# All embedding gathers on GpSimd, with seven tiles for gathered rows instead of two

## The chip, the cores and the metric

The kernel runs on one core of a Trainium2 chip. The metric is the device time of one execution in microseconds (us). Such a core has five engines that run side by side: TensorE (PE in the profile: matrix products and transposes), VectorE (DVE), ScalarE (ACT), GpSimd (POOL) and SyncE (SP, which here only issues transfers). Transfers between the chip's memory and the core's on-chip memory are done by 16 DMA engines; SyncE, ScalarE and GpSimd each have a queue on which they issue them.

## The reference, cut to what matters

A spiking recommender: each of 1024 users has 50 items, the rows of an embedding table that belong to them are averaged as a running prefix, normalised over the batch, run through a leaky integrate-and-fire neuron, and the mean spike count is scored against the whole table.

```python
emb = emb_table.at[0].set(0.0)             # 100001 x 128
e = emb[seq]                               # seq: 1024 x 50
prefix = jnp.cumsum(e, axis=1)
denom = jnp.minimum(t_idx[None, :], lengths[:, None])
uF = prefix / denom[:, :, None]
mean, var = uF.mean(axis=0), uF.var(axis=0)     # over the batch
y = (uF - mean) * lax.rsqrt(var + BN_EPS) * gamma + beta

def step(v, x):                            # scanned over the 50 steps
    v = v + (x - v) / TAU
    spike = (v - V_TH >= 0)
    return v - spike * V_TH, spike

scores = spikes.mean(axis=0) @ emb.T       # 1024 x 100001
```

## The kernel before

The kernel has two stages. The first computes the spike counts, 128 features by 1024 users; the second multiplies them with the whole table and writes 409.6 MB of scores.

**First stage, 50 steps.** Step t needs the rows of the table that the 1024 users have at place t. `gather(t)` (L201) takes a tile of 128 x 1024 and issues eight indirect transfers from GpSimd, one for each block of 128 users: each fetches 128 rows of 128 numbers, one row into each partition. The tiles come from the pool `gather`, which has two buffers. For four of the steps, 44 to 47, the first of the eight blocks is not gathered by GpSimd: it lies in a tile of its own, `aside[t]` (128 x 128). These four tiles are filled early by SyncE (L184 to L197): for each of the 128 partitions it reads four indices into registers and issues four transfers of one row (512 transfers of 0.5 KB), behind the loads of the indices, lengths and constants and the first six groups of table rows on the same queue. The gather loop then starts at block 1 for these steps (`range(t in aside, NB)`).

In the loop over t (L300), `gather(t + 1)` is issued first. TensorE transposes the eight blocks of step t and adds them onto the running prefix, which stays in two PSUM banks, `pre` (L313). For each half of the users VectorE scales the prefix by the length (L322) and takes its statistics (L323). Both halves' statistics give the mean and variance (L333), ScalarE and a few small VectorE instructions the scale (L337 to L352), ScalarE the normalised value (L338, L356), and VectorE the neuron's step, spike and reset (L343, L359, L365). TensorE adds a correction for item 0 (L270) and sums the spikes (L281). Step t + 1 can't have its neuron's step before step t has, so these form a recurrence beside the gathers. The order of work on each engine is that of the program; waits between engines follow from the tiles that are read and written.

At the end of steps 42 and 44 (L371 to L373) the first two blocks of 1024 table rows are prepared for the second stage: TensorE transposes them, ScalarE writes a rounded copy `hi`, VectorE the remainder `lo`. The four tiles for these, `hi0`, `lo0`, `hi1` and `lo1` (128 x 1024, pool `embT`), are taken at the start of the program (list `free`, L76) and are not used before step 42. In the last step VectorE computes the counts, and the first two blocks of scores are multiplied, scaled and stored (L396 to L408), the first of them in a tile of the pool `gather`.

At the start two more tiles of the pool `gather` serve other ends: `isz` (where an item is 0, L217) and `rb` (the lengths' reciprocals, L239), each transposed once by TensorE.

**Second stage.** For chunks of 2 to 6 blocks of 1024 table rows and for each of eight blocks of users, TensorE multiplies counts with `hi` and `lo`, VectorE and ScalarE take turns at moving the products to an output tile, and SyncE stores it (L427 to L493). The output tiles of the second stage lie where the tiles of the first stage lay.

Of the kernel before, what the change touches and what calls it, by code (L numbers as in the profile page):

```python
# [12 lines left out]
F32 = mybir.dt.float32  # L13
BF16 = mybir.dt.bfloat16
F32R = mybir.dt.float32r
# [5 lines left out]
P = 128  # L21
BN_EPS = 1e-5
V_TH = 1.0
HALF = 1024
KQ = HALF // P
BANK = 512
# [8 lines left out]
def rec_kernel(  # L35
# [9 lines left out]
    nc = tc.nc  # L45
    B, T = seq.shape
    N, D = table.shape
    NB = B // P
# [24 lines left out]
    rows = {}  # L73
    split = {}

    free = [  # L76
        [embp.tile([P, HALF], F32R, tag=f"{x}{i}", name=f"{x}_{i}") for x in ("hi", "lo")] for i in range(2)
    ]

    def size(q):  # L80
        return min(HALF, N - q * HALF)
# [79 lines left out]
    with ExitStack() as ph:  # L161
# [1 line left out]
        lp = ph.enter_context(tc.tile_pool(name="lif", bufs=2))  # L163
        sp = ph.enter_context(tc.tile_pool(name="stats", bufs=3))
        up = ph.enter_context(tc.tile_pool(name="uF", bufs=2))
        gp = ph.enter_context(tc.tile_pool(name="gather", bufs=2))
        accp = ph.enter_context(tc.tile_pool(name="acc", bufs=1, space=bass.MemoryType.PSUM))
        vp = ph.enter_context(tc.tile_pool(name="v", bufs=1, space=bass.MemoryType.PSUM))

# [11 lines left out]

        aside = {}  # L184
        for t0, many in ((T - 6, 4),):
            for t in range(t0, t0 + many):
                aside[t] = once.tile([P, P], F32, tag=f"aside{t}", name=f"aside_{t}")
            for p in range(P):
                _, items = nc.values_load_multi_w_load_instructions(
                    idx[p : p + 1, 0, t0 : t0 + many],  # L190
                    engines=[mybir.EngineType.SP],
                    min_val=0,
                    max_val=N - 1,
                    skip_runtime_bounds_check_because="items are rows of the table; the transfer checks its own bounds",
                )
                for j, item in enumerate(items):
                    nc.sync.dma_start(out=aside[t0 + j][p : p + 1, :], in_=table[bass.ds(item, 1), :])  # L197

        es = {}

        def gather(t):  # L201
            es[t] = gp.tile([P, B], F32, tag="e", name=f"e_{t}")
            for n in range(t in aside, NB):
                nc.gpsimd.indirect_dma_start(  # L204
                    out=es[t][:, n * P : (n + 1) * P],
                    out_offset=None,
                    in_=table,
                    in_offset=bass.IndirectOffsetOnAxis(ap=idx[:, n, t : t + 1].bitcast(U32), axis=0),
                )

        make_identity(nc, ident)
        gather(0)

        isz = gp.tile([P, NB, P], F32, tag="e", name="isz")  # L217
        nc.vector.memset(isz, 0.0)
        for u in (0, P // 2):
            nc.vector.tensor_single_scalar(isz[:, :, u : u + T], idx, 0.0, ALU.is_equal)  # L220
# [15 lines left out]
        rl = once.tile([P, NB], F32, tag="rl", name="rl")  # L236
        nc.vector.tensor_copy(rl, len_i)
        nc.vector.reciprocal(rl, rl)
        rb = gp.tile([P, NB, P], F32, tag="e", name="rb")  # L239
        nc.vector.tensor_copy(rb, rl.unsqueeze(2).to_broadcast([P, NB, P]))  # L240
        rps = vp.tile([P, B], F32, tag="v0", name="rps")
        for n in range(NB):
# [56 lines left out]
        l = only(1)  # L299
        for t in range(T):  # L300
            last = t == T - 1
            if t + 1 < T:
                gather(t + 1)
            e = es.pop(t)
            if last:
                s = lp.tile([P, B], BF16, tag="s", name=f"s_{t - 1}")
                nc.vector.tensor_single_scalar(s, v, V_TH, ALU.is_ge)
                nc.vector.tensor_tensor(negv, s, v, ALU.subtract)
            uF = up.tile([P, B], F32, tag="uF", name=f"uF_{t}")
            bs = sp.tile([P, B // BANK, 6], F32, tag="bs", name=f"bs_{t}")  # L310
            for h, cs in enumerate(halves):
                for k in range(0, BANK, P):
                    nc.tensor.matmul(  # L313
                        pre[h][:, k : k + P],
                        lhsT=aside[t] if h == k == 0 and t in aside else e[:, h * BANK + k : h * BANK + k + P],
                        rhs=ident,
                        start=False,
                        stop=last,
                        is_transpose=True,
                        skip_group_check=True,  # L320
                    )
                nc.vector.scalar_tensor_tensor(uF[:, cs], rlen[:, cs], 1.0 / (t + 1), pre[h], ALU.max, ALU.mult)  # L322
                nc.vector.bn_stats(bs[:, h, :], uF[:, cs])  # L323
            if not last:
                correct(t + 1, l)
            else:

                counted(t - 1, s)
                count = once.tile([P, B], F32, tag="zT", name="count")
                for h, cs in enumerate(halves):  # L330
                    nc.scalar.copy(count[:, cs], sums[h])
            mv = sp.tile([P, 2], F32, tag="mv", name=f"mv_{t}")
            nc.vector.bn_aggr(mv, bs.rearrange("p h s -> p (h s)"))  # L333


            r = sp.tile([P, 1], F32, tag="r", name=f"r_{t}")
            nc.scalar.activation(r, mv[:, 1:2], AF.Sqrt, bias=eps)  # L337
            nc.scalar.activation(uF, uF, AF.Identity, bias=mv[:, 0:1], scale=-1.0)  # L338


            if t and not last:
                s = lp.tile([P, B], BF16, tag="s", name=f"s_{t - 1}")
                nc.vector.tensor_single_scalar(s, v, V_TH, ALU.is_ge)  # L343
                counted(t - 1, s)

            nc.vector.reciprocal(r, r)
            q = sp.tile([P, 1], F32, tag="q", name=f"q_{t}")
            nc.vector.tensor_mul(q, r, r)
            nc.vector.scalar_tensor_tensor(q, mv[:, 1:2], BN_EPS, q, ALU.add, ALU.mult)
            nc.vector.tensor_scalar(q, q, -0.5, 1.5, ALU.mult, ALU.add)  # L350
            a = sp.tile([P, 1], F32, tag="a", name=f"a_{t}")
            nc.vector.tensor_scalar(a, q, r, hgb[:, 0:1], ALU.mult, ALU.mult)  # L352


            def x(vt, cs):
                nc.scalar.activation(vt, uF[:, cs], AF.Identity, bias=hgb[:, 1:2], scale=a)  # L356

            def step(vt, cs):
                nc.vector.scalar_tensor_tensor(vt, negv[:, cs], -0.5, vt, ALU.mult, ALU.add)  # L359

            if not last:
                vt = vp.tile([P, B], F32, tag=f"v{t % 2}", name=f"v_{t}")
                x(vt, whole)
                if t:
                    nc.vector.tensor_tensor(negv, s, v, ALU.subtract)  # L365
                step(vt, whole)
                v = vt
                if t + 2 < T:
                    l = only(t + 2)

                if t in (T - 8, T - 6):  # L371
                    q = (t - T + 8) // 2
                    prepare(q, vp.tile([P, HALF], F32, tag="v1", name=f"pt_{q}"))  # L373


# [20 lines left out]


        po1 = vp.tile([P, HALF], F32, tag="v0", name="po_0_1")
        for q, (pool, tag, po) in enumerate(((gp, "e", sums), (up, "uF", [po1[:, cs] for cs in halves]))):
            o = pool.tile([P, HALF], F32, tag=tag, name=f"o_0_{q}")  # L400
            for h, cs in enumerate(halves):
                product(po[h], q, 0, h * BANK, BANK)
# [110 lines left out]
```

## Time and profile before

| | |
|---|---|
| median of three runs | 1776.87 us |
| lowest and highest run | 1771.08 and 1780.48 us |
| profiled execution, span from first to last instruction | 1569.9 us |
| time of the profiled execution beyond its span | not given by the page |
| instructions | 14231 |
| TensorE, VectorE, ScalarE, GpSimd busy | 1153.1, 940.7, 630.6, 374.6 us |
| gathers on GpSimd | 396, 373.9 us busy, 944 ns each |
| mean transfer rate | 311 GB/s |
| HBM read and written | 77.69 and 409.60 MB |

All of these except the runs' times come from one execution, recorded by the hardware profiler. The page cuts its span into 40 slices and gives the busy share of each engine in tenths. It lists the costliest groups of instructions by line, and the chain of work that ended last: from the last instruction back, at each step to what released it. "issue" is time in which an engine waited for nothing that the profile shows. A row in order of time has the start, the duration, the engine, the line, what is written and read, and in brackets the idle time before it and what ended it.

### The profile page before, as it was taken

How to read it: one execution, taken by the hardware profiler on the slowest of the kernel's cores; microseconds unless marked ns; L12 is line 12 of the kernel's file. 1: busy time of each engine (PE TensorE's matmuls, PEld its weight loads, DVE VectorE, ACT ScalarE, POOL GpSimd, SP SyncE). 2: the span in 40 equal slices, each digit the busy share in tenths (PEclk: the TensorE clock that was granted, in tenths of full speed). 3: DMA queues.
4: the chain of work that ended last, by engine and by line, in shares of the span. 5: the costliest groups of instructions: out<-in, count | busy, mean ns of one | idle time of the engine just before them, and what ended most of it. 6: DMA issues, size and time to landing. Idle time of an engine off the chain costs nothing.

```text
span 1569.9 us, 14231 instructions
## 1 busy us (share of the span) xinstructions
PE 1153.1 (73%) x4548; PEld 822.3 (52%) x4548; DVE 940.7 (60%) x1161; ACT 630.6 (40%) x700; POOL 374.6 (24%) x402
## 2 busy tenths in 40 slices
PE   4555555555556988899878788887788888788784
PEld 2222222222233766677666666666666666666563
DVE  4777777777778665576545555555555545555453
ACT  2322222222233554465444444444444444444342
POOL 6777777777775000000000000000000000000000
PEclk7555555555555999999999988999999998989998
DMA  9622222222222999999999999999999999999998
GB/s 342 245 55 53 55 54 54 54 53 54 52 53 64 399 411 420 420 393 428 425 432 427 429 428 424 418 422 424 428 413 420 415 424 429 421 423 409 394 423 354
DMA packets 54600, 488.25 MB, mean 311 GB/s; under 512 B 12443, under 2 KB 13756, under 8 KB 33276
## 3 DMA queue, kind: packets, MB, share of 16 engines
q1 hardware_dynamic: 33008, 429.03, 65.1%
q0 software_dynamic: 12672, 25.98, 6.2%
q10 hardware_dynamic: 8844, 32.33, 5.2%
q8 instruction: 36, 0.59, 0.1%
q14 instruction: 40, 0.33, 0.1%
HBM read 77.69 MB, written 409.60 MB: 310 GB/s over the span
## 4 chain that ended last, share of the span: by engine, by line
DMA 52%; POOL 17%; PE 11%; issue 9%; ACT 5%; DVE 4%; DVEq 0%; ACTq 0%; SPq 0%; POOLq 0%
DMA scores<-o 49%; POOL e L204 17%; PE po L149 9%; ACT o L473 5%; DMA e<-in_L_rec_emb_table,idx 3%; DVE o L471 2%; PE pt L119 1%; DVE bs L323 1%; DVE uF L322 0%; DVE s L343 0%; PE pre L313 0%; PE sums L281 0%; DMA idx<-in_r_seq 0%; ACT hi L141 0%; ACT pairs L141 0%
## 5 line engine op out<-in xcount | busy, mean ns | idle before, releaser
L471 DVE TENSOR_SCALAR o<-po 128x1024 f32<-128x1024 f32 x391 | 463.5, 1220 | 351.8 <-DMA scores<-o 323.4
L473 ACT ACTIVATE o<-po 128x1024 f32<-128x1024 f32 (+1 forms) x391 | 387.9, 1018 | 547.8 <-DMA scores<-o 344.9
L204 POOL DMA_INDIRECT e<-in_L_rec_emb_table,idx x396 | 373.9, 944 | 123.4 <-issue 114.6
L149 PE MATMUL po<-pairs,countB 128*128 128x512 f32 x1168 | 314.7, 415 | 67.6 <-ACT o L473 50.7
L149 PEld LDWEIGHTS po<-pairs,countB 128*128 128x128 f32 x1168 | 225.8, 198 | 132.5 <-ACT o L473 65.8
L149 PE MATMUL po<-pairs,countC 128*128 128x512 f32 x876 | 239.1, 419 | 43.6 <-ACT o L473 43.6
L313 PE MATMUL pre<-ident,e 128*128 128x128 f32 x396 | 153.1, 450 | 143.8 <-DMA e<-in_L_rec_emb_table,idx 142.2
L149 PEld LDWEIGHTS po<-pairs,countC 128*128 128x128 f32 x876 | 170.1, 200 | 89.7 <-ACT o L473 54.7
L313 PEld LDWEIGHTS pre<-ident,e 128*128 128x128 f32 x396 | 78.5, 201 | 236.1 <-DMA e<-in_L_rec_emb_table,idx 214.7
L142 DVE TENSOR_TENSOR pairs<-pt,pairs 128x1024 fp32r<-128x1024 f32 (+1 forms) x73 | 88.3, 1217 | 96.6 <-ACT pairs L141 96.5
L337 ACT ACTIVATE r<-mv,eps 128x1 f32<-128x1 f32 x50 | 14.7, 295 | 300.6 <-DVE mv L333 300.6
L322 DVE SCALAR_TENSOR_TENSOR uF<-rlen,pre 128x512 f32<-128x512 f32 x100 | 68.3, 683 | 103.8 <-PE pre L313 103.8
L119 PE MATMUL pt<-ident,rows 128*128 128x128 f32 x782 | 113.5, 293 | 8.0 <-ACT o L473 3.9
L119 PEld LDWEIGHTS pt<-ident,rows 128*128 128x128 f32 x782 | 102.6, 154 | 28.8 <-issue 10.0
L149 PE MATMUL po<-hi,countB 128*128 128x512 f32 x200 | 82.8, 414 | 18.8 <-ACT o L473 13.8
L281 PE MATMUL sums<-s,ident_h 128*128 128x512 bf16 x98 | 49.6, 608 | 60.6 <-DVE s L343 60.6
L270 PE MATMUL pre<-zT,l 128*128 128x512 f32 x100 | 78.0, 782 | 21.6 <-DVE uF L322 21.5
L149 PE MATMUL po<-lo,countB 128*128 128x512 f32 x200 | 80.4, 402 | 0.0
L141 ACT CAST pairs<-pt 128x1024 fp32r<-128x1024 f32 (+1 forms) x73 | 73.6, 1008 | 16.2 <-PE pt L119 15.9
L149 PE MATMUL po<-pairs,countA 128*128 128x512 f32 (+1 forms) x292 | 73.2, 393 | 9.1 <-ACT o L473 9.1
L149 PE MATMUL po<-hi,countC 128*128 128x512 f32 x150 | 62.7, 418 | 16.4 <-ACT o L473 16.4
L356 ACT ACTIVATE v<-uF,hgb,a 128x1024 f32<-128x1024 f32 x49 | 59.2, 1208 | 37.4 <-DVE a L352 37.4
(78 smaller groups left out, 821.1 us busy)
## 6 DMA issues: line engine op xcount, KB each, us to landing
scores<-o SPq DMA_DIRECT2D x96, 3072.0 KB
scores<-o SPq DMA_DIRECT2D x32, 1536.0 KB
rows<-in_L_rec_emb_table ACTq DMA_DIRECT2D x20, 1536.0 KB
scores<-o SPq DMA_DIRECT2D x22, 1024.0 KB
rows<-in_L_rec_emb_table SPq DMA_DIRECT2D x6, 3072.0 KB
scores<-o SPq DMA_DIRECT2D x8, 2048.0 KB
scores<-o SPq DMA_DIRECT2D x8, 1872.5 KB
aside<-in_L_rec_emb_table SPq DMA_DIRECT2D x512, 0.5 KB
```

What stands on the lines that cost most here:

```text
L119: nc.tensor.transpose(pt[:, k0 : k0 + kw], r[:kw, k0 : k0 + D], ident[:kw, :kw])
L141: nc.scalar.copy(vh, vp)
L142: nc.vector.tensor_tensor(vl, vp, vh.bitcast(F32), ALU.subtract)
L149: nc.tensor.matmul(po[:, :kw], lhsT=counts[n], rhs=part[:, k0 : k0 + kw], start=j == 0, stop=j == 1,)
L204: nc.gpsimd.indirect_dma_start(out=es[t][:, n * P : (n + 1) * P], out_offset=None, in_=table, in_offset=bass.IndirectOffsetOnAxis(ap=idx[: ...
L270: nc.tensor.matmul(pre[h], lhsT=l, rhs=zT[:, h * BANK : (h + 1) * BANK], start=t == 0, stop=False, skip_group_check=True,)
L281: nc.tensor.matmul(sums[h], lhsT=ident_h, rhs=s[:, h * BANK : (h + 1) * BANK], start=t == 0, stop=t == T - 2, skip_group_check=True,)
L313: nc.tensor.matmul(pre[h][:, k : k + P], lhsT=aside[t] if h == k == 0 and t in aside else e[:, h * BANK + k : h * BANK + k + P], rhs=ident ...
L322: nc.vector.scalar_tensor_tensor(uF[:, cs], rlen[:, cs], 1.0 / (t + 1), pre[h], ALU.max, ALU.mult)
L356: nc.scalar.activation(vt, uF[:, cs], AF.Identity, bias=hgb[:, 1:2], scale=a)
L471: nc.vector.tensor_scalar_mul(o[:, h0 : h0 + hw], po[:, :hw], 1.0 / T)
L473: nc.scalar.mul(o[:, h0 : h0 + hw], po[:, :hw], 1.0 / T)
```

## The change

All 400 gathers (50 steps of eight) are issued by GpSimd. The four aside tiles, the 512 transfers and the reading of indices into SyncE's registers are gone. The tiles for gathered rows are now these: `e0`, `e1` and `e2` of the pool `gather` (one buffer each), and the four tiles `hi0`, `lo0`, `hi1` and `lo1`, which would lie empty until step 42. Steps 0 to 42 go round all seven in the order of the list `deep`; steps 43 to 49 go round `e1`, `e2`, `e0`. `gathers(t)` issues, ahead of step t, every gather whose tile's former holder has been read by a step before t: six steps ahead in the first part, two in the last. Before the loop, the first five gathers are issued into `e0`, `hi0`, `lo0`, `hi1`, `lo1`. `isz` now lies in `e1` and `rb` in `e2`. `pair(q)` takes the tiles `hi` and `lo` at steps 42 and 44, where the blocks are prepared. The first output tile lies in `e0`.

```diff
-    free = [
-        [embp.tile([P, HALF], F32R, tag=f"{x}{i}", name=f"{x}_{i}") for x in ("hi", "lo")] for i in range(2)
-    ]
+    free = []
+
+    def pair(i):
+        free.append([embp.tile([P, HALF], F32R, tag=f"{x}{i}", name=f"{x}_{i}") for x in ("hi", "lo")])
...
-        gp = ph.enter_context(tc.tile_pool(name="gather", bufs=2))
+        gp = ph.enter_context(tc.tile_pool(name="gather", bufs=1))
...
-        aside = {}
-        for t0, many in ((T - 6, 4),):
-            for t in range(t0, t0 + many):
-                aside[t] = once.tile([P, P], F32, tag=f"aside{t}", name=f"aside_{t}")
-            for p in range(P):
-                _, items = nc.values_load_multi_w_load_instructions(
-                    idx[p : p + 1, 0, t0 : t0 + many],
-                    engines=[mybir.EngineType.SP],
...
-                for j, item in enumerate(items):
-                    nc.sync.dma_start(out=aside[t0 + j][p : p + 1, :], in_=table[bass.ds(item, 1), :])
-
+        deep = ["e0", "hi0", "lo0", "hi1", "lo1", "e1", "e2"]
+        flat = T - len(deep)
+        slots = [deep[t % len(deep)] for t in range(flat)]
+        slots += [f"e{(t - flat + 1) % 3}" for t in range(flat, T)]
         es = {}
+        held = {}
 
         def gather(t):
-            es[t] = gp.tile([P, B], F32, tag="e", name=f"e_{t}")
-            for n in range(t in aside, NB):
+            tag = slots[t]
+            pool = gp if tag[0] == "e" else embp
+            es[t] = pool.tile([P, B], F32, tag=tag, name=f"e_{t}")
+            held[tag] = t
+            for n in range(NB):
                 nc.gpsimd.indirect_dma_start(
...
+        to_gather = 0
+
+        def gathers(t):
+            nonlocal to_gather
+            while to_gather < T and held.get(slots[to_gather], -1) < t:
+                gather(to_gather)
+                to_gather += 1
+
         make_identity(nc, ident)
-        gather(0)
-        isz = gp.tile([P, NB, P], F32, tag="e", name="isz")
+        isz = gp.tile([P, NB, P], F32, tag="e1", name="isz")
+        rb = gp.tile([P, NB, P], F32, tag="e2", name="rb")
+        while slots[to_gather] != "e1":
+            gather(to_gather)
+            to_gather += 1
+
...
-            if t + 1 < T:
-                gather(t + 1)
+            gathers(t)
...
-                        lhsT=aside[t] if h == k == 0 and t in aside else e[:, h * BANK + k : h * BANK + k + P],
+                        lhsT=e[:, h * BANK + k : h * BANK + k + P],
...
                 if t in (T - 8, T - 6):
                     q = (t - T + 8) // 2
+                    pair(q)
                     prepare(q, vp.tile([P, HALF], F32, tag="v1", name=f"pt_{q}"))
...
-        for q, (pool, tag, po) in enumerate(((gp, "e", sums), (up, "uF", [po1[:, cs] for cs in halves]))):
+        for q, (pool, tag, po) in enumerate(((gp, "e0", sums), (up, "uF", [po1[:, cs] for cs in halves]))):
```

More of the change, by code (lines that the diff above doesn't have):

```diff
@@ L180, in rec_kernel @@
             fetch(group(g), g * GROUP, GROUP)
-        aside = {}
-        for t0, many in ((T - 6, 4),):
-            for t in range(t0, t0 + many):
-                aside[t] = once.tile([P, P], F32, tag=f"aside{t}", name=f"aside_{t}")
-            for p in range(P):
-                _, items = nc.values_load_multi_w_load_instructions(
-                    idx[p : p + 1, 0, t0 : t0 + many],
-                    engines=[mybir.EngineType.SP],
[L192 to L195, printed above, removed]
-                for j, item in enumerate(items):
-                    nc.sync.dma_start(out=aside[t0 + j][p : p + 1, :], in_=table[bass.ds(item, 1), :])
+        deep = ["e0", "hi0", "lo0", "hi1", "lo1", "e1", "e2"]
+        flat = T - len(deep)
+        slots = [deep[t % len(deep)] for t in range(flat)]
+        slots += [f"e{(t - flat + 1) % 3}" for t in range(flat, T)]
         es = {}
+        held = {}
         def gather(t):
-            es[t] = gp.tile([P, B], F32, tag="e", name=f"e_{t}")
-            for n in range(t in aside, NB):
+            tag = slots[t]
[3 more added lines that the diff above has]
+            for n in range(NB):
                 nc.gpsimd.indirect_dma_start(
```

1 line of the change is left out of this document (removed).

## The prediction

> **What bounds the kernel now.** I first read the page's head, its slices and its costliest groups. The two stages stand apart there: a first third in which GpSimd (POOL) is the steadily busy engine, and the rest, in which the DMA engines are full.
>
> ```profile
> span 1569.9 us, 14231 instructions
> ...
> POOL 6777777777775000000000000000000000000000
> ...
> DMA  9622222222222999999999999999999999999998
> ...
> L204 POOL DMA_INDIRECT e<-in_L_rec_emb_table,idx x396 | 373.9, 944 | 123.4 <-issue 114.6
> ```
>
> A slice is 1569.9 / 40 = 39.2 us. POOL stops in the thirteenth, near 500 us; from then on the DMA engines write scores. The group of gathers has 396 of them (50 steps of 8, less the 4 that SyncE fetches), 944 ns each. POOL never counts as more than seven tenths busy, so the next question is what its idle time before a gather is. That is the view of who waited for whom, for POOL up to 560 us:
>
> ```profile
> POOL e L204 <- issue: 114.6, 376, 0.3
> POOL e L204 <- DMA e<-in_L_rec_emb_table,idx: 3.4, 11, 0.3
> POOL e L204 <- DMA idx<-in_r_seq: 3.0, 1, 3.0
> POOL e L204 <- PE pre L313: 2.4, 8, 0.3
> ```
>
> The only wait longer than 0.3 us is the first, for the indices. All others are 0.3 us long whatever they are put down to: 114.6 / 376 = 0.305 us where nothing released the gather, 2.4 / 8 = 0.30 us where TensorE's reading of the tile did, 3.4 / 11 = 0.31 us for an earlier gather. So 0.30 us is the pitch of POOL's own instruction stream, and POOL has never stood still for a free tile. Two tiles are already enough. The order in time gives the pitch:
>
> ```profile
> 4.30 1.16 POOL L204 DMA_INDIRECT e<-in_L_rec_emb_table,idx  x1 [2.99 <-DMA idx<-in_r_seq]
> ...
> 497.64 0.94 POOL L204 DMA_INDIRECT e<-in_L_rec_emb_table,idx  x1 [0.30 <-issue]
> ```
>
> These are the first and the 396th gather: (497.64 - 4.30) / 395 = 1.249 us for each, 9.99 us for a step of eight. The last gather of step 48 is the 388th (49 x 8 - 4), and starts at 4.30 + 387 x 1.249 = 487.7 by this pitch. Now the chain of waits where the first stage ends, which tells if the gathers or the recurrence comes last:
>
> ```profile
> 487.65 2.48 DMA e<-in_L_rec_emb_table,idx
> 490.18 0.49 PE pre L313
> 490.69 0.70 DVE uF L322
> ...
> 495.73 1.24 DVE v L359
> 496.99 1.24 DVE s L307
> 498.25 1.22 DVE negv L308
> 499.47 0.61 DVE uF L322
> 500.11 0.69 DVE bs L323
> 500.80 0.67 DVE uF L322
> ...
> 528.44 8.76 DMA scores<-o
> ```
>
> The last gather of step 48 is issued at 487.65 us, lands 2.48 us later, is transposed, and VectorE (DVE) takes up its half at 490.69. From there the chain is the recurrence of steps 48 and 49 on DVE: 500.80 - 490.69 = 10.11 us to the second half of step 49. It then goes by way of the final counts and products to the stores, which come last at each step from 528.44 us on. Everything after 490.69 hangs on the moment at which step 48's rows have landed.
>
> **The change, part by part.** *Four gathers more.* In steps 44 to 47 POOL gathers eight blocks instead of seven. All four come ahead of step 48's last gather, which becomes the 392nd. At 1.249 us each this is 4 x 1.249 = 5.0 us: it starts at 487.65 + 5.0 = 492.65 and DVE takes up its half at 490.69 + 5.0 = 495.69. Nothing covers it, since POOL issues without a break. The price was never seen for these four blocks, so bounds: at the least only the busy 0.944 us each, 3.8 us; at the most the first gather's 1.16 us and a gap of 0.31 each, 5.9 us. I take 5.0, the mean of 395 rows of the same instruction.
>
> [...]
>
> *Does the recurrence keep up, so that the 5.0 us arrive whole?* It has to be looked at where the two table blocks are prepared (L372 and L373, steps 42 and 44), since these delay it. The starts of DVE's second half, step by step from 43:
>
> ```profile
> 447.82 0.67 DVE L322 SCALAR_TENSOR_TENSOR uF<-rlen,pre 128x512 f32<-128x512 f32 x1
> ...
> 455.31 0.67 DVE L322 SCALAR_TENSOR_TENSOR uF<-rlen,pre 128x512 f32<-128x512 f32 x1
> ...
> 465.75 0.67 DVE L322 SCALAR_TENSOR_TENSOR uF<-rlen,pre 128x512 f32<-128x512 f32 x1
> ...
> 473.23 0.67 DVE L322 SCALAR_TENSOR_TENSOR uF<-rlen,pre 128x512 f32<-128x512 f32 x1
> ```
>
> The recurrence by itself needs 7.48 us (473.23 - 465.75), with a block to prepare 10.44 (465.75 - 455.31). With eight gathers in each step, step 44's last one is the 360th, at 4.30 + 359 x 1.249 = 452.69; rows ready for DVE 2.48 + 0.49 and some 0.07 later, 455.7. Step 45 is the recurrence's: 455.7 + 10.4 = 466.1 (its rows: 465.7). Step 46: recurrence 473.6, rows 475.7. Step 47: rows, 485.7; step 48: rows, 495.7. So after the second preparation the gathers lead again by step 46. Step 49: recurrence 495.7 + 10.1 = 505.8, rows 505.7. Either way 5.0 us later than 500.80.
>
> *Seven tiles up to step 42.* They let POOL run up to six steps ahead, but POOL is the engine that is behind: a step takes it 9.99 us and the recurrence 7.48 us. TensorE empties each tile about as soon as it lands. The price lies between the 2.4 + 3.4 = 5.8 us of waits on tiles above, if all of it vanished, and nothing; I take nothing, because these waits are as long as those without a releaser.
>
> *Three tiles from step 43.* A gather of step t waits for TensorE's reading of step t - 3. The tightest is the last preparation: step 48's gathers start at 492.65 - 7 x 1.249 = 483.9 and need step 45's rows read, which is before 466.1 by the sum above. 17 us of cover; price nothing. If the recurrence fell more than that behind, each further us would come through whole. Behind such a gather only later gathers are queued on POOL.
>
> *The pairs hi and lo as gather tiles.* They serve steps 1 to 4, 8 to 11, ... 36 to 39; the preparation at step 42 writes hi0 and lo0 five steps after TensorE read step 37. Price nothing; it would need 50 us of lateness.
>
> *SyncE without its 512 small transfers.* Its queue in order of time:
>
> ```profile
> 3.83 33.42 SPq L97 DMA_DIRECT2D rows<-in_L_rec_emb_table  x6
> 38.04 318.47 SPq L197 DMA_DIRECT2D aside<-in_L_rec_emb_table  x512
> 506.78 53.00 SPq L158 DMA_DIRECT2D scores<-o  x26
> ```
>
> They end at 38.04 + 318.47 = 356.5 us; the next thing on that queue is issued at 506.78. Ahead of them stand the row fetches, which they can't delay. In their time DMA is two tenths busy. They are worth nothing at the end; what SyncE saves becomes waiting.
>
> *Where things lie.* The output tiles of the second stage take the space of the first stage's. The aside tiles' 2048 bytes go, so the uF tiles move down by as much and lie more under the second block's output tile; a third gather tile comes behind. Before, one evacuation there already waited for a store:
>
> ```profile
> 511.46 1.22 DVE L471 TENSOR_SCALAR o<-po 128x1024 f32<-128x1024 f32 x1 [1.47 <-DMA scores<-o]
> ```
>
> What TensorE did just then, in the chain:
>
> ```profile
> 512.81 8.27 PE po L149 x36
> ```
>
> TensorE set the pace there, so the 1.47 us cost nothing. By the tile sizes (once some 18 KB, then 4 KB of spikes, 2 KB of statistics, then uF) the second output tile already overlapped the first uF tile by some 600 bytes, so this wait stays what it was; I take nothing, and up to a store's 8.76 us (chain above) less the 1.47 us as the other end.
>
> **Sum.** 5.0 us on a span of 1569.9: 1574.9. The page gives the profiled execution no time beyond its span. The median of the three runs is 1776.87, 207.0 us more; I carry that over as it is, since nothing in the trace says what it is made of. 1776.87 + 5.0 = 1781.9, or 0.28%. The three runs lie 9.4 us apart. A difference of 0.5%, 8.9 us, is about what a measurement of this kernel can tell from no change.
>
> **The rivals.** *A, the gathers are hidden (1776 to 1777).* DVE works from 495.73 to the second half of step 49 without a gap, so it could be the recurrence that ends last, and four gathers more would cost near 0; with the 5.8 us of tile waits returned it is 1776.87 + 5.0 - 5.8 = 1776.1. [...] Against it: the chain enters the recurrence by a landing at 490.18, and the landing moves. Chance 0.15.
>
> *B, slower: an output tile waits for a store (1789).* Place: the second and third block of the first chunk, right behind 511 us. If the moved uF tiles make their evacuation wait for a full store, it is 8.76 - 1.47 = 7.3 us on top of 5.0, 1776.87 + 12.3 = 1789.2. It decides from the point where the wait is longer than what TensorE still has to do for other blocks (PSUM tiles in hand). For it: the 1.47 us wait exists and the tiles move. Against: the same two tiles met before. Chance 0.12.
>
> *C, faster: the small transfers were late in the timed runs.* 207 us of the median are in no view. If SyncE's transfers took longer there than 318.47 us, step 44 would wait for them. They have 94 us to spare (356.5 to step 44 at 451 us, between the rows 447.82 and 455.31), so it decides from 1.3 times their time here; at the most it is all of 207 us, 1781.9 - 207.0 = 1574.9. Against: no view shows this queue held up by anything but its own 512 issues. Chance 0.05.
>
> *D, the change doesn't do what it says.* The seven tiles are never filled ahead: that is what I forecast, and costs no time beside it.
>
> **How the numbers follow.** The forecast 0.65, A 0.15, B 0.12, C 0.05, and 0.03 for what I don't see. Within 0.5%: A, and nine tenths of the forecast (its 5.0 us lie 3.9 under the bound, and medians can be off by that), with the rest of it and B slower: same 0.75, slower 0.18, faster 0.07. The range goes from 7 under A's 1776 to 6 over B's 1789, the spread of the runs: 1769 to 1795.
>
> **What would show it.** Right: 400 gathers of 944 ns, pitch 1.249; the last at 4.30 + 399 x 1.249 = 502.7; first store at 506.78 + 5.0 = 511.8; span near 1574.9; no POOL wait above 0.3 us but the first. A: first store still near 507. B: a DVE or ACT wait on a store of over 5 us before 535. A longer gap between gathers would be an error of mine: 0.01 us each is 4 us. Wrong at all: a POOL wait for TensorE of microseconds after step 43.

## The result

| | before | after |
|---|---|---|
| median | 1778.67 us (1771.08 to 1781.21, 4 runs) | 1674.85 us (1672.07 to 1678.04, 4 runs) |
| profiled execution | span 1569.9 us, own time not given | span 1670.3 us, own time 1672.07 us |

The change makes the kernel faster: the ratio is 0.9423, with an interval of 0.9398 to 0.9448. Forecast was 1781.9 us, a little slower. The time lies 94 us below the forecast's lowest bound.

The spans of the two profiles tell the opposite, 100 us more after than before. The span after lies 1.8 us under its own run, so it belongs to the timed runs; the span before lies 201 us under even the lowest of its timed runs and does not. All that follows rests on one thing: the kernel before runs in one of two conditions, about 1571 us in some sets of runs and about 1780 us in others, all runs of a set agreeing, and the two profiles shown so far are of different ones. I call them the short and the long condition; times are only compared within one.

The page of the kernel after, its head, slices and groups:

```profile
span 1670.3 us, 12572 instructions
...
POOL 7766666667645600000000000000000000000000
...
DMA  9511111111111149999999999999999999999998
...
L198 POOL DMA_INDIRECT e<-in_L_rec_emb_table,idx x400 | 377.9, 945 | 206.8 <-issue 113.3
...
L322 DVE SCALAR_TENSOR_TENSOR uF<-rlen,pre 128x512 f32<-128x512 f32 x100 | 67.9, 679 | 195.8 <-remote 173.7
```

A gather takes what it took, 945 ns against 944. But POOL goes on through the fourteenth slice, of 41.8 us each (to 585 us), and its idle time has grown from 123.4 to 206.8 us. VectorE's first instruction of each half step, L322, now waits 195.8 us in all; 173.7 of them end by "remote", which means that the signal which ended the wait is recorded, but no instruction that ended shortly before it. SyncE's queue in order of time shows where the first stage ends:

```profile
3.63 33.30 SPq L98 DMA_DIRECT2D rows<-in_L_rec_emb_table  x6
606.19 1052.37 SPq L159 DMA_DIRECT2D scores<-o  x172
```

The first store is at 606.19 us. From there to the end it is 1670.3 - 606.2 = 1064.1 us, before it was 1569.9 - 506.8 = 1063.1. The second stage has not moved; the whole question is the first. Who waited for whom on POOL:

```profile
POOL e L198 <- issue: 113.3, 372, 0.3
POOL e L198 <- remote: 62.8, 16, 8.1
POOL e L198 <- PE pre L313: 24.7, 1, 24.7
```

Outside these the gathers follow each other as before (0.3 us each). But POOL now does stand still for tiles: 62.8 us in 16 waits, and once 24.7 us for TensorE. To see why, here is what TensorE does in the fourth and fifth step, in order of time:

```profile
58.91 1.91 PE L313 MATMUL pre<-ident,e 128*128 128x128 f32 x8
78.54 0.76 PE L271 MATMUL pre<-zT,l 128*128 128x512 f32 x1 [17.72 <-DVE uF L322]
89.65 0.79 PE L271 MATMUL pre<-zT,l 128*128 128x512 f32 x1 [10.35 <-DVE uF L322]
...
92.51 1.91 PE L313 MATMUL pre<-ident,e 128*128 128x128 f32 x8
```

and VectorE in the same stretch:

```profile
60.34 1.23 DVE L359 SCALAR_TENSOR_TENSOR v<-negv,v 128x1024 f32<-128x1024 f32 x1 [0.21 <-ACT v L356]
77.71 0.69 DVE L322 SCALAR_TENSOR_TENSOR uF<-rlen,pre 128x512 f32<-128x512 f32 x1 [16.13 <-remote]
...
88.91 0.69 DVE L322 SCALAR_TENSOR_TENSOR uF<-rlen,pre 128x512 f32<-128x512 f32 x1 [9.79 <-remote]
```

The eight transposes of step 3 are recorded as done at 58.91 + 1.91 = 60.82 us. VectorE is free at 61.57. It takes up the first half at 77.71 and the second at 88.91. For 16 and 10 us nothing works on this step: the rows are there, the transposes are done, and word of it arrives late. The signal itself is in the trace: the semaphore that VectorE waits for, one that TensorE counts up, is updated at 77.68 us, 0.03 us before VectorE starts. So the signal is late, not VectorE. From the recorded end of the transposes to VectorE's start it is 16.9 us here for the first half (77.71 - 60.82), where in the chain that the prediction shows it is 0.02 us (490.69 - 490.18 - 0.49).

The lateness seems to belong to the time in which gathers are issued. POOL once stands still, from 484.95 to 509.69 us:

```profile
484.01 0.94 POOL L198 DMA_INDIRECT e<-in_L_rec_emb_table,idx  x1 [0.30 <-issue]
509.69 0.94 POOL L198 DMA_INDIRECT e<-in_L_rec_emb_table,idx  x1 [24.74 <-PE pre L313]
```

and TensorE's transposes of steps 38 to 40, which fall into this pause, come one recurrence apart:

```profile
492.55 1.91 PE L313 MATMUL pre<-ident,e 128*128 128x128 f32 x8
...
500.02 1.92 PE L313 MATMUL pre<-ident,e 128*128 128x128 f32 x8
...
507.51 1.91 PE L313 MATMUL pre<-ident,e 128*128 128x128 f32 x8
```

7.47 and 7.49 us, the recurrence by itself, with no late signal. This alone proves little, since one or two such steps in a row also occur while POOL gathers; the five in a row from step 38 to 42 are the only such stretch before step 43. An experiment below leaves the gathers out.

### The profile page after: what moved, and what is told of

It reads as the page before. It is cut to its first block, busy times and chain, and to the rows that moved or that the text cites. A ratio compares the mean times of both kernels' runs of the same rounds, so it can differ in the third digit from the quotient of the medians.

```text
span 1670.3 us, 12572 instructions
## 1 busy us (share of the span) xinstructions
PE 1111.4 (67%) x4548; PEld 830.0 (50%) x4548; DVE 940.2 (56%) x1161; ACT 630.7 (38%) x700; POOL 378.6 (23%) x406
## 4 chain that ended last, share of the span: by engine, by line
DMA 48%; DVE 20%; another core or an unknown queue 11%; PE 9%; ACT 5%; issue 4%; POOL 2%; DVEq 0%; ACTq 0%; SPq 0%; POOLq 0%
DMA scores<-o 47%; PE po L150 8%; ACT o L474 4%; DVE bs L323 4%; DVE uF L322 3%; DVE v L359 3%; DVE s L343 3%; DVE negv L365 2%; POOL e L198 2%; DVE o L472 2%; DMA e<-in_L_rec_emb_table,idx 1%; DVE a L352 1%; ACT v L356 1%; DVE mv L333 1%
## 5 line engine op out<-in xcount | busy, mean ns | idle before, releaser
L198 POOL DMA_INDIRECT e<-in_L_rec_emb_table,idx x400 | 377.9, 945 | 206.8 <-issue 113.3
L271 PEld LDWEIGHTS pre<-zT,l 128*128 128x128 f32 x100 | 28.0, 281 | 331.6 <-issue 217.6
L322 DVE SCALAR_TENSOR_TENSOR uF<-rlen,pre 128x512 f32<-128x512 f32 x100 | 67.9, 679 | 195.8 <-remote 173.7
L313 PE MATMUL pre<-ident,e 128*128 128x128 f32 x400 | 99.6, 421 | 11.6 <-DMA e<-in_L_rec_emb_table,idx 9.7
L313 PEld LDWEIGHTS pre<-ident,e 128*128 128x128 f32 x400 | 86.1, 226 | 38.7 <-issue 24.1
L150 PE MATMUL po<-hi,countC 128*128 128x512 f32 x150 | 62.8, 419 | 16.2 <-ACT o L474 16.1
```

What stands on the lines that cost most here:

```text
L150: nc.tensor.matmul(po[:, :kw], lhsT=counts[n], rhs=part[:, k0 : k0 + kw], start=j == 0, stop=j == 1,)
L198: nc.gpsimd.indirect_dma_start(out=es[t][:, n * P : (n + 1) * P], out_offset=None, in_=table, in_offset=bass.IndirectOffsetOnAxis(ap=idx[: ...
L271: nc.tensor.matmul(pre[h], lhsT=l, rhs=zT[:, h * BANK : (h + 1) * BANK], start=t == 0, stop=False, skip_group_check=True,)
L313: nc.tensor.matmul(pre[h][:, k : k + P], lhsT=e[:, h * BANK + k : h * BANK + k + P], rhs=ident, start=False, stop=last, is_transpose=True, ...
```

## The experiments

All are kernels for the same table and users. The runs fell into five sets; in each the kernel before was run beside them. "Long" and "short" say which condition the set had.

### Does the kernel before show it too? (long: before 1780.93, 1776.86 to 1788.52)

The kernel before, unchanged:

> The kernel before, unchanged, profiled beside its own timed runs. In the profile of after TensorE's signals come late in stretches: VectorE waits 173.7 us at L322 with nothing to wait for but transposes that the records show as done. Theory L (late signals belong to the executions that are timed, and the first profile of before happened to be free of them): a span of about 1770 us, a first stage that ends near 700 instead of 507 us, and waits of VectorE at L322 some 200 us longer than the 103.8 us of the first profile. Theory S (SyncE's 512 small transfers are what is late): the span about 1770 us too, but one long wait of TensorE at step 44 for the tile aside, and L322 otherwise as in the first profile. If the first profile stands for the timed runs: span 1570 us, and neither theory.

Measured: 1780.98 us, ratio 0.9988 (0.9966 to 1.0009), with a profile whose span, 1781.2 us, fits it. Its SyncE queue in order of time:

```profile
38.95 615.10 SPq L197 DMA_DIRECT2D aside<-in_L_rec_emb_table  x512
716.27 1053.11 SPq L158 DMA_DIRECT2D scores<-o  x172
```

The 512 small transfers take 615.10 us instead of 318.47. They end at 654.05, and step 44 needs them. POOL gathers until about 528 us and then stands still until 656. In two stretches, from its start to 500 us and from 530 to 654 us, the same queue reads:

```profile
38.95 460.87 SPq L197 DMA_DIRECT2D aside<-in_L_rec_emb_table  x269
...
529.90 124.14 SPq L197 DMA_DIRECT2D aside<-in_L_rec_emb_table  x214
```

460.87 / 269 = 1.71 us each while POOL gathers; 124.14 / 214 = 0.58 us each while it stands still. In the short condition it was 318.47 / 512 = 0.62 us with the gathers running. What step 44 does, on TensorE:

```profile
524.71 1.01 PE L281 MATMUL sums<-s,ident_h 128*128 128x512 bf16 x2 [1.26 <-issue]
653.87 0.45 PE L313 MATMUL pre<-ident,aside 128*128 128x128 f32 x1 [128.14 <-DMA aside<-in_L_rec_emb_table]
```

and the waits of the first 720 us:

```profile
DVE uF L322 <- remote: 179.3, 39, 10.6
...
POOL e L204 <- PE pre L313: 129.7, 3, 127.1
PE pre L313 <- DMA aside<-in_L_rec_emb_table: 128.1, 1, 128.1
```

TensorE stands 128.1 us for the small transfers, and POOL, out of tiles, stands with it for 127.1. Beside that the late signals are there as well (179.3 us, all waits of L322 by "remote", those that other work covers among them). The first stage ends 716.3 - 506.8 = 209.5 us later than in the short condition: 128 for the small transfers, some 81 that are left, put down here to late signals. This is, but for some 2 us, the 207 us that the prediction carried over.

### The change's two parts apart

Only the small transfers taken out; two tiles as before (long, same set):

```diff
-        aside = {}
...
-                    nc.sync.dma_start(out=aside[t0 + j][p : p + 1, :], in_=table[bass.ds(item, 1), :])
-            for n in range(t in aside, NB):
+            for n in range(NB):
-                        lhsT=aside[t] if h == k == 0 and t in aside else e[:, h * BANK + k : h * BANK + k + P],
+                        lhsT=e[:, h * BANK + k : h * BANK + k + P],
```

> Before without SyncE's 512 transfers: 400 gathers on GpSimd, still two tiles. Theory L: each late stretch stops the gathers too, as they have no free tile, so the time stays near before plus four gathers, 1777 + 5 = 1782 us. Theory S: the transfers were the loss, so the time falls to that of after, about 1675 us, with two tiles as well.

Measured: 1653.31 us (1652.96 to 1653.69), ratio 0.9274 (0.9242 to 0.9307). Its store queue and its waits:

```profile
587.09 1052.75 SPq L158 DMA_DIRECT2D scores<-o  x172
```

```profile
DVE uF L307 <- remote: 134.9, 25, 8.7
...
POOL e L189 <- remote: 62.2, 15, 4.4
```

1780.98 - 1653.31 = 127.7 us faster than before, which is the wait at step 44; the first store is 716.27 - 587.09 = 129.2 us earlier. This is more than the whole change brings. The late signals stay: the first store is at 587.1, and between 511.1 and 512.5 in the nine traces of the short condition with the same 400 gathers, so some 75 us earlier.

Only the seven tiles; SyncE fetches small rows as before, though for three steps instead of four (long, same set):

```diff
+        aside = {}
+        for t0, many in ((T - 6, 3),):
...
-            for n in range(NB):
+            for n in range(t in aside, NB):
...
-                        lhsT=e[:, h * BANK + k : h * BANK + k + P],
+                        lhsT=aside[t] if h == k == 0 and t in aside else e[:, h * BANK + k : h * BANK + k + P],
```

> After with SyncE's small transfers put back for three of the four steps (384 transfers; four tiles of rows beside seven for gathers don't fit in the memory): seven tiles, 397 gathers on GpSimd. Theory L: the gain of after comes from the tiles, so about 1675 us. Theory S: the transfers cost most of the difference, 384/512 of 104 us, so about 1750 us.

Measured: 1761.74 us (1759.39 to 1767.25), ratio 0.9889 (0.9849 to 0.9929). SyncE's queue and the waits of the first 720 us:

```profile
39.54 600.13 SPq L198 DMA_DIRECT2D aside<-in_L_rec_emb_table  x384
695.46 1052.50 SPq L159 DMA_DIRECT2D scores<-o  x172
```

```profile
POOL e L213 <- PE pre L328: 110.4, 4, 80.7
...
PEld pre L328 <- DMA aside<-in_L_rec_emb_table: 82.6, 1, 82.6
```

With a quarter fewer transfers they still need 600 us, and step 44 still waits for them, 82.6 us; without them the same seven tiles take some 86 us less (1675.93 in another set). So the gain of the change comes from SyncE's transfers, and seven tiles on top of that cost some 21 us (1674.85 or 1675.93 against 1653.31, from different sets).

### Is it the gathers that make the rest late?

In the kernels of this pair no step from step 8 on gathers: steps 8 to 49 use the rows of steps 6 and 7 by turns, so the scores are not those of the reference, and 336 of the 400 gathers are left out (332 of 396 where SyncE fetches its rows).

```diff
+        held = {}
...
         def gather(t):
+            if t >= 8:
+                es[t] = held[t % 2]
+                return
             es[t] = gp.tile([P, B], F32, tag="e", name=f"e_{t}")
+            held[t % 2] = es[t]
...
```

Each was executed once in a set. They were first run in a set where the kernel before took 1571.5 us (short), and nothing is late there:

> Two tiles, no small transfers, and no gathers from step 8 on: the recurrence goes on with the rows of steps 6 and 7, so this leaves 336 of the 400 gathers out. It asks whether gathers under way make TensorE's signals late. Theory G (they do: TensorE's signals and SyncE's instructions share something with the gathers): from step 9 on no step longer than the recurrence's 7.48 us except at the two preparations, VectorE takes up the last half 2.4 us after the last transpose in each, and the first stage ends near 90 + 41 x 7.48 + 6 + 12 = 415 us. Rival P (TensorE's signals are late by themselves, every few steps): steps of 15 to 19 us go on, as in the kernel with two tiles.

Measured: 1482.85 us, first store 417.11.

> The kernel before with its 512 small transfers, and no gathers from step 8 on (the recurrence goes on with the rows of steps 6 and 7). Theory G: SyncE's transfers go at 0.58 us each from some 90 us on, as they did in the run of before once the gathers stood still, so they end near 90 + 470 x 0.58 = 365 us, before step 44 asks for them (near 395 us), and nothing waits. Rival Q (SyncE's transfers are slow by themselves in timed runs): they take some 600 us again, and step 44 waits for over 200 us.

Measured: 1482.99 us, small transfers 318.66 us long, first store 417.06. Neither can speak on lateness. Run once more where before took 1778.03 us (long; 1769.2 to 1780.11):

> Two tiles, no small transfers, no gathers from step 8 on (336 of 400 left out; the recurrence goes on with the rows of steps 6 and 7). Only on a chip where before takes 1780 us does it tell: theory G (gathers under way make TensorE's signals late): late signals end with the gathers, steps of 7.48 us from step 9 on, first store near 440 us (417 on the other chip, and some 20 us lost in the first eight steps). Rival P (the signals are late by themselves): steps of 15 to 19 us go on, first store beyond 480 us. Where before takes 1571 us: 417 us again.

Measured: 1494.07 us, first store 428.39: 11 us over the short condition, all of it from the first 93 us, in which there are gathers. VectorE's waits for late signals, here at L312, in these 93 us, and then its longest waits from there to the first store:

```profile
DVE uF L312 <- remote: 25.9, 4, 11.2
...
DVE v L349 <- ACT v L346: 9.3, 43, 0.5
DVE lo L142 <- ACT hi L141: 4.9, 2, 3.1
```

No late signal is left after the last gather. From step 6 on the steps take 7.5 us, but for those behind the preparation of a block of the table and the last one, as in the short condition.

> Before with its 512 small transfers, no gathers from step 8 on. Where before takes 1780 us: theory G: SyncE's transfers go at 0.58 us each once the gathers are over (near 100 us), end near 380 us, and step 44 doesn't wait. Rival Q (they are slow by themselves there): they take some 600 us, and step 44 waits over 200 us. Where before takes 1571 us: 318 us for them, as seen.

Measured: 1494.55 us. SyncE's queue, whole, and then cut at the end of the last gather, near 93 us:

```profile
37.89 338.65 SPq L197 DMA_DIRECT2D aside<-in_L_rec_emb_table  x512
428.72 1052.27 SPq L158 DMA_DIRECT2D scores<-o  x172
...
37.89 54.01 SPq L197 DMA_DIRECT2D aside<-in_L_rec_emb_table  x25
...
93.33 283.21 SPq L197 DMA_DIRECT2D aside<-in_L_rec_emb_table  x487
```

338.65 us instead of 615.10, with the same 512 transfers in the long condition, and no wait at step 44: 54.01 / 25 = 2.16 us each beside gathers, 283.21 / 487 = 0.58 us each without. Theory G holds (the gathers make SyncE's instructions and TensorE's signals late), and its rivals, that SyncE's queue or TensorE's signals are slow by themselves in this condition, fall. What of a gather does it, its issue on GpSimd, its landing or the recording of either, these runs don't tell apart.

### How many tiles?

Three tiles in the pool of gathers, no small transfers (taken out as above), nothing in `hi` and `lo`:

```diff
-        gp = ph.enter_context(tc.tile_pool(name="gather", bufs=2))
+        gp = ph.enter_context(tc.tile_pool(name="gather", bufs=3))
...
```

> Two tiles and no small transfers gave 1653 us, seven tiles 1675. Here are three, all in the pool gather. If the depth of the gathers' lead is what costs the 21 us (they run on while TensorE's signals stand): between the two, some 1655 to 1662 us. If it is where the tiles lie (hi and lo): 1653 us.

Measured in the short condition (before 1571.5, 1570.77 to 1572.17): 1576.36 us, ratio 1.0031 (1.0019 to 1.0042).

Two tiles, but in the places `hi0` and `lo0` up to step 41, then `e0` and `e1`:

```diff
-        deep = ["e0", "hi0", "lo0", "hi1", "lo1", "e1", "e2"]
-        flat = T - len(deep)
+        deep = ["hi0", "lo0"]
+        flat = T - 8
-        slots += [f"e{(t - flat + 1) % 3}" for t in range(flat, T)]
+        slots += [f"e{(t - flat) % 2}" for t in range(flat, T)]
...
-        while slots[to_gather] != "e1":
-            gather(to_gather)
-            to_gather += 1
+        gather(0)
+        to_gather = 1
```

> No small transfers, two tiles at any time, but up to step 41 these are hi0 and lo0; from step 42 on e0 and e1. If the depth costs: 1653 us as with two tiles in the pool gather. If it is where the tiles lie: about 1675 us.

Measured, same set: 1576.09 us, ratio 1.0028 (1.0017 to 1.004). In the short condition neither number nor place matters; both cost what four gathers more cost.

In the long condition (before 1778.03):

> The changed kernel, unchanged. The runs so far fall in two conditions by the chip they were on: before takes 1571 us on one and 1780 us on the other, where TensorE's signals and SyncE's instructions come late. Where before takes 1571 us: gathers bind, four more cost 4 x 1.249 us, so 1576.5 us, seven tiles or two. Where before takes 1780 us: 1675 us, as in the result. If seven tiles cost something by themselves: over 1580 us on the first.

Measured: 1675.93 us (1671.53 to 1678.73), ratio 0.9423 (0.9387 to 0.9459), first store 611.54. This expectation laid the condition to the chip. That is wrong: the chip of this set is the one that had given the short condition before.

> 400 gathers, three tiles in the pool gather. Where before takes 1780 us: if the lead of the gathers costs the 21 us between two tiles (1653) and seven (1675), some 1655 to 1662 us; if it is the place of the tiles, 1653 us. Where before takes 1571 us: 1576 us again.

Measured: 1651.42 us (1651.03 to 1652.2), ratio 0.9291 (0.9261 to 0.9322). If the lead were what costs, a price for the third tile was expected; there is none in the time. By its own expectation this run speaks for the place of the tiles and against the lead. Its store queue:

```profile
585.31 1053.28 SPq L158 DMA_DIRECT2D scores<-o  x172
```

This is the best version that was run in the long condition, 1.5% under the changed kernel of the same set (1651.42 / 1675.93). In the short condition it is level with it, and the kernel before is the fastest there.

Whether seven tiles cost their 21 to 24 us by GpSimd's lead or by where they lie was asked twice more, together with four and five tiles (`deep` cut to `e0, hi0, e1, e2` and to `e0, hi0, lo0, e1, e2`, `flat = T - 10`). Both sets came in the short condition (before 1571.5 and 1571.11), so the question was not answered:

> All 400 gathers on GpSimd, no small transfers; rows in hi0 and lo0 by turns up to step 41, then in e0 and e1. Theory L (what the seven tiles cost is their lead: GpSimd runs up to six steps ahead at the start): with the kernel before near 1780 us beside it, about 1653 us, as two tiles in the pool of gathers, first store near 587 us. Rival P (it is the place, the tiles hi and lo): about 1675 us, first store near 608. With the kernel before near 1571 us beside it both say 1576, and nothing is told apart.

Measured: 1576.3 us, ratio 1.0031 (1.002 to 1.0043).

> All 400 gathers on GpSimd, rows in e0, hi0, e1 and e2 up to step 39, then in e0, e1, e2: four tiles, so a lead of three steps. With the kernel before near 1780 us beside it: theory L says a price between three tiles (1651) and seven (1675), in proportion to the lead 1651 + 24 x 1/4 = 1657 us; rival P says 1651 + 24 x 1/4 = 1657 as well if a tile costs by its share, and 1675 if any tile in hi costs all. With the kernel before near 1571 us: 1576 by both.

Measured: 1576.16 us, ratio 1.0029 (1.0018 to 1.004).

> All 400 gathers on GpSimd, rows in e0, hi0, lo0, e1 and e2 up to step 39, then in e0, e1, e2: five tiles, a lead of four steps. With the kernel before near 1780 us beside it: theory L in proportion to the lead 1651 + 24 x 2/4 = 1663 us; if only the flood at the start counts, nearly all of it is still there, since it takes GpSimd 50 us to fill five tiles: about 1665. Rival P: 1665 to 1675. With the kernel before near 1571 us: 1576 by both.

Measured: 1576.29 us, ratio 1.003 (1.0019 to 1.0042).

> As two_tiles_in_hi_lo_2, whose chip ran the kernel before in 1571.5 us, so that nothing was told apart. If the kernel before takes about 1780 us beside it this time: theory L (the lead) about 1653 us and a first store near 587, rival P (the place) about 1675 and near 608. Beside 1571: 1576 again.

Measured: 1576.26 us, ratio 1.0032 (1.002 to 1.0043).

> As four_tiles. Beside a kernel before of about 1780 us: theory L 1657 us (1651 + 24 x 1/4), first store near 592; rival P 1657 to 1675. Beside 1571: 1576 again.

Measured: 1576.26 us, ratio 1.0032 (1.002 to 1.0045).

> As five_tiles. Beside a kernel before of about 1780 us: theory L 1663 us (1651 + 24 x 2/4), first store near 598; rival P 1663 to 1675. Beside 1571: 1576 again.

Measured: 1576.49 us, ratio 1.0033 (1.002 to 1.0045).

What the traces of the long condition show of the lead is this (start of the second half, DVE at L322 or its like):

| kernel | end of POOL's first unbroken run | step 5 | step 42 | step 49 | first store |
|---|---|---|---|---|---|
| two tiles | 34 us | 83.35 | 498.87 | 580.83 | 587.09 |
| three tiles | 54 us | 87.89 | 509.47 | 579.05 | 585.31 |
| seven tiles (after) | 114 us | 139.97 | 526.37 | 599.93 | 606.19 |

With seven tiles POOL issues without a break for 114 us before it first has to wait for a tile, and for as long VectorE's halves come late: step 3 takes 33.6 us and step 4 32.9 us. At step 5 the kernel is 139.97 - 83.35 = 56.6 us behind two tiles. It makes 29.1 of these good up to step 42 (10.44 us a step against 11.23) and 8.4 more up to step 49, which leaves 19.1 us, the difference of the first stores. That the lead at the start is to blame fits this; it is argued from traces, not shown by a run. Three tiles fit it only in part: at step 42 they are 10.6 us behind two tiles, but make it good over the last seven steps and end ahead. The rival, that the places `hi` and `lo` cost, was not tested in the long condition, and stands.

### The change in the short condition

> The changed kernel once more, on the chip of the three runs above. With the kernel before near 1780 us beside it: 1675 us, as twice before. With the kernel before near 1571 us beside it, where its time has not been seen yet: by the prediction's own sum 1571.5 + 5.0 = 1576.5, slower than before by 0.3%; that would show that the whole gain belongs to the condition in which SyncE's transfers are late.

Measured: 1576.31 us (1576.03 to 1577.21) beside a kernel before of 1571.5 us (1570.86 to 1572.28), ratio 1.0031 (1.0018 to 1.0044). The page, POOL's waits, and its last gather:

```profile
span 1574.4 us, 12572 instructions
...
POOL 6777777777775000000000000000000000000000
```

```profile
POOL e L198 <- issue: 118.2, 388, 0.3
POOL e L198 <- DMA idx<-in_r_seq: 2.7, 1, 2.7
POOL e L198 <- DMA e<-in_L_rec_emb_table,idx: 2.1, 7, 0.3
POOL e L198 <- PE pre L313: 0.9, 3, 0.3
```

```profile
502.31 0.95 POOL L198 DMA_INDIRECT e<-in_L_rec_emb_table,idx  x1 [0.30 <-issue]
```

```profile
511.52 1051.16 SPq L159 DMA_DIRECT2D scores<-o  x172
```

Here the change makes the kernel slower by 4.8 us. No wait of POOL but the first is over 0.3 us, the last gather starts at 502.31, the first store is issued at 511.52. The whole gain of the change belongs to the long condition.

## Why the prediction was wrong, point by point

**Four gathers more, 5.0 us: right, in the condition of the profile that it was read from.** The pitch of 1.249 us gave 502.7 for the last gather, 511.8 for the first store and 1574.9 for the span. The trace of the short condition has 502.31, 511.52 and 1574.4, and the times rise by 4.8 us (1571.5 to 1576.31).

**The recurrence, the tiles' space, three tiles at the end: right there too.** Two, three, four, five and seven tiles, in either place, all give 1576.1 to 1576.5 us. No wait on a store before 540 us is over 1.5 us in the trace of the changed kernel there.

**Seven tiles, nothing: right in the short condition, wrong in the long.** There POOL does get ahead, 77 us at step 5 and still 62 to 71 us through most of the loop (gather issued to rows taken up), because TensorE's signals are late; and where three tiles took 1651.42 us, seven took 1675.93. The prediction's signal for "wrong at all", a POOL wait for TensorE of microseconds after step 43, came at that place: 24.7 us, ahead of the gathers of step 43, the first of the three-tile part. It did not cost what it seems to: meanwhile the steps ran at 7.48 us.

**SyncE's transfers, nothing: this is one of two steps that failed.** They were priced by 318.47 us from the one trace, with 94 us to spare. In a trace of the kernel before that fits the timed runs (before_again, 1782.93 us) they take 615.10 us and step 44 waits 128.1 us for them. Taking them out brings 127.7 us.

**The 207 us carried over: the other, and the root of it.** The prediction saw that the profiled execution and the timed runs lay 207 us apart and went on as if the same kernel had been profiled plus a constant. It was not a constant: 128 of it was a wait that the change removes, and some 81 are signals that come late while gathers run, which the change leaves and by its seven tiles raises by about 20, whether by their number or by their place. By the runs the sum is 1778.67 - 127.7 (the four gathers already in it) + 22.6 (1675.93 - 1653.31, from two sets) = 1673.6, against 1674.85 measured. Whether the four gathers cost 5.0 us in the long condition too, no run separates.

**Rival C had the mechanism** ("the small transfers were late in the timed runs", decided from 1.3 times their time; they took 1.93 times), at a chance of 0.05. It gave the most that this can bring as 207 us. The transfers were worth some 128, since the late signals are a second cost of the same condition. Against it stood "no view shows this queue held up", but all views were of the other condition: absence from that trace was no evidence, and this was the only rival that explained the 207 us at all. **A** falls (the 4.8 us are there), **B** falls, **D** is false in the long condition: the tiles are filled ahead.

What stays open: what puts a set of runs into the one condition or the other. The chip alone doesn't, since one chip gave both. TensorE's granted clock doesn't: of the kernel before, one execution took 1571.5 us at a mean clock of 0.807 and another 1784.13 us at 0.813. Why seven tiles cost more than three is open too, as told above.

## What to carry to other kernels

Before a profile is used, its own span has to be reconciled with the timed runs: a gap of 207 us on 1777 is more than any version here with all its gathers gained (some 128 us), and a range that doesn't cover what the gap may be made of is a range for another execution. Something with slack in one trace (here 94 us on a queue of small transfers) has to be priced for the case that the slack is not there, above all where it consists of many instructions on a queue that shares its time with gathers. More buffers ahead of an engine that already keeps pace can cost: in the long condition three tiles did all that seven did, and 24 us better, though it is open whether the number of the seven or their place is to blame.

## What the runs showed of the hardware

- While GpSimd issued gathers at 1.249 us each, other engines' signals came late in the long condition without any engine working longer. SyncE's transfers took 1.71 us each in the kernel before, against 0.58 us once the gathers stood still and 0.62 in the short condition. In step 3 of the changed kernel TensorE's finished transposes reached VectorE 16.9 and 28.1 us after their recorded end (from 60.82 to 77.71 and to 88.91). Both ended within microseconds of a pause in the gathers: the last gather before the kernel before's pause is issued at 528.07 us, and from 529.90 on SyncE's transfers took 0.58 us; TensorE's signals caught up 6.9 us into a pause of POOL, as told below. GpSimd's own pitch stayed at 1.249 us in the changed kernel, VectorE's 128x512 scaling at 679 ns (683 in the short condition). TensorE's signals then came on a fixed grid: in the changed kernel the updates of its semaphore between 47 and 138 us lie multiples of 0.70 us apart, to within 0.02 us (62.98, 67.18, 69.98, 74.88, 77.68 among them), and after POOL had stood still from 131.73 us on, six came 0.03 us apart (138.58 to 138.75). In the profile of the kernel before, in the short condition, an update follows the recorded end of its transpose by 0.01 us (490.67 after 490.66).
- The records of the two conditions differ as well. Each of the eight semaphores that gathers signal has 786 to 802 events in the trace of the kernel before in the short condition, 16 for each of its 49 or 50 gathers and at most two more; in the long condition the changed kernel, with 50 gathers on each, left 107 to 282 of them. That records were lost there is a guess, which no run tests; if recording also holds up the signals, the lateness would be one of recorded executions only. All runs of the experiments are recorded executions, so none can tell.
- In the short condition the same kernel repeats within 0.1% (the kernel before between 1570.66 and 1572.28); in the long one before spreads over 1769.2 to 1788.5.
